# A four-layer graph kernel: attention prepared with Newton steps and early tiles, 64x64 maps in layer 2, biases moved to the head

## The chip, the cores and the metric

The kernel runs on one core of a Trainium2 chip. The metric is the device time of one execution in microseconds (us), taken as the median of three runs. Beside it stands one profiled execution, from which every duration of a single instruction comes.

## What is computed

Eight graphs (B) of 2048 nodes (N) with 64 features (F) pass through four residual layers that share one 0/1 adjacency matrix `adj` (2048 x 2048). Each layer first norms every node's features and clips them at zero. Cut to what matters here:

```
h = relu(layernorm(x))                      # before every layer
# layer 0: hyperedges and neighbours
industry = (adj / deg) @ (h @ W_ind)        # deg: row sums of adj
agg      = softmax over members (...) @ hW  # one vector per hyperedge
g        = weighted sum over a node's hyperedges of elu(mix of hW and agg)
x       += softmax-weighted mix of industry and g
# layer 1: graph attention
x       += elu(softmax(leaky(s_src + s_dst), masked by adj) @ hW)
# layer 2: three steps
v = relu(W1 [v, adj @ v] + b1);  v = W2 v + b2      # x 3, then x += v
# layer 3: Chebyshev terms and per-node weights
x += sum over k of T_k(adj) h @ w[node, k] + embedding @ bias
```

## The kernel before, in words

Two graphs are packed in one 128-partition tile (`half(0)` and `half(1)`), so there are four pairs `p`; nodes are cut in 16 tiles of 128 (`m`) or 4 chunks of 512 columns (`c`). TensorE (PE) does all contractions; a product with the adjacency is split in a rounded part and a rest (`hi`, `lo`), each one pass of 512 columns. Plain fp32 products appear as two instructions each.

The order of the work comes from three sources. Engines wrapped in `InOrder` (V, A, G, S for VectorE, ScalarE, GpSimd and SyncE) and all `kit.mm` while `kit.strict` is set keep the order of the program. Everything else is placed by the tile scheduler. In layers 2 and 3 a small planner (`Weave`) starts side chains when a planned time has passed.

The stages, with the lines of the profile:

- **Head of layer 0** (`layer0`, `step(j - lag)`): per node tile load `x`, norm on VectorE, GpSimd and ScalarE, transpose (L743), map with `W_ind` (L736 `py`), split, and `spread` the tile into four accumulators for chunk 0 of `industry`. Six 0.5 MB adjacency tiles `at` (L945, issued by GpSimd) are asked for before the loop.
- **Industry, chunks 1 to 3** (`industry`, `out_of`, `members`): 16 node tiles times 8 products `acc<-at,Y` (L1060). Between them, one per half tile, stand the `units`: the members of the hyperedges (`ph` L1115, copies `hi` L1119 and `lo` L1120, weights `es` L1123 to L1125, `hs` L1126, `pg` L1138), listings and, at the end, tables and the layer-3 biases (`pb` L1225, copy L1227). The row sums of the adjacency are added up on VectorE (`ds`, L1068), which the scheduler places; after the last product they are summed over partitions (`deg`, L1080), inverted with Ln and Exp (L1087, L1088) and multiplied into the copied accumulators (`ev`, L1075, L1091).
- **Pairs** (the loop `for j in range(last + 2 * NB)`): 54 steps over node and hyperedge pairs. VectorE does `mix`, `mix + pa` and `ex`, ScalarE an Exp, GpSimd the weighting (`weighed`), PE the products `pd`, `pa`, `pgs`. Before the loop stand the first tile's `ranks`, `edges`, `turn`, `shares` and the copies of the input into `x1_dram`.
- **Output of layer 0** (16 chunks; `first`, `second`, `third`, `differ`, `fourth`): two products with `fcW` (`pf`, 64-row tiles), Tanh to `th_s` (1024 columns), their difference, a product `pd` (64-column tiles), Tanh, and the mix `df`, which is added to `x1_dram` by an accumulating DMA for `p` over 0. `iv` (L1477) is loaded back from `ind_dram`; three 1 MB accumulating DMAs `xd<-hn` (L1536) add `gT`. Between these steps `first_neighbours` prepares pair 0 of layer 1: mean, variance (Square, PE, Ln, Exp), maps `ph`, scores, row factors `R`.
- **Attention, layer 1** (`attend`): per pair, half and node tile two VectorE passes `pt` (L1739, 128x1024), then 8 products `o` and 4 products `dn` on 32-column tiles. The next pair's preparation is woven in.
- **Layers 2 and 3** (`layers23`): per pair three steps of four chunks; each chunk is one map of `v` (`acc<-v,W1v` or `acc<-v,Wvc`, 128x128 stationary matrix with two equal 64x64 blocks on its diagonal), then 32 passes `acc<-aT,parts` (`spread`), a ReLU (L2089), and the map `py` for the next step (`carry`, `moved`). Then layer 3 with `u` (64-row tiles) and the reductions on VectorE.

Of the kernel before, what the change touches and what calls it, by code (L numbers as in the profile page):

```python
# [16 lines left out]
P = 128  # L17
# [602 lines left out]
LN_EXP = "natural_log_exp_and_others"  # L620

# [14 lines left out]
class Kit:  # L636


    def __init__(self, tc, t, pool):
# [11 lines left out]
        self.eps = pool.tile([P, 1], FP, name="eps_f")  # L651
        nc.vector.memset(self.eps, EPS)

        self.tiny = pool.tile([P, 1], FP, name="tiny_f")
        nc.vector.memset(self.tiny, 1e-30)
# [117 lines left out]
def layer0(kit, hn, x1_dram, open_early, late_tile, between):  # L773
# [31 lines left out]
    rden = lst.tile([P, LT, B], FP, name="rden")  # L805

# [28 lines left out]
    with ExitStack() as sA:  # L835
# [35 lines left out]
        def listing(ps):  # L871
# [4 lines left out]
            def slots():  # L876
                tmp = lst.tile([P, SLOTS], mybir.dt.int32, tag="hhi", name="iota_i", bufs=3)
                nc.gpsimd.iota(tmp, pattern=[[1, SLOTS]], base=0, channel_multiplier=0)
# [3 lines left out]
                nc.gpsimd.iota(ti, pattern=[[1, P]], base=0, channel_multiplier=-1)  # L882
# [51 lines left out]
        sp = sA.enter_context(tc.tile_pool(name="streamf", bufs=6, reuse_waits="tile"))  # L934
# [16 lines left out]
        with ExitStack() as s1:  # L951
            sb = s1.enter_context(tc.tile_pool(name="nf_sb", bufs=2, reuse_waits="tile"))
            ps = s1.enter_context(tc.tile_pool(name="nf_ps", bufs=2, space=PSUM, reuse_waits="tile"))
            acc = accs()
# [9 lines left out]
            def sums(i):  # L964
                st[i] = sb.tile([P, 2, B], FP, tag="st", name="st", bufs=4)
                V.tensor_reduce(st[i][:, 0], groups(xs[i]), AX.X, OP.add)
                V.tensor_scalar(st[i][:, 0], st[i][:, 0], -1.0 / F, None, op0=OP.mult)
# [47 lines left out]
            for i in range(4):  # L1015
                load(i)
            for g in range(6):
                at[g] = rows_of(0, g)
            kit.strict = True
            for j in range(NT + 5):  # L1020
                on = lambda k: 0 <= j - k < NT
                if 0 < j and j + 3 < NT:
                    load(j + 3)
                if j == 6:
                    first = loads()
                for lag, step in (
# [3 lines left out]
                    if on(lag):  # L1030
                        step(j - lag)
                m = j - 5
                if m > 0 and m % 2 and m // 2 + 6 < NT // 2:
                    at[m // 2 + 6] = rows_of(0, m // 2 + 6)
# [6 lines left out]
        with ExitStack() as s1:  # L1041
# [7 lines left out]
            def industry(c, own):  # L1049
# [3 lines left out]
                acc, ds = accs(), dsp.tile([P, 2, CW], FR, tag="ds", name="ds")  # L1053
                for g in range(NT // 2):
                    at = rows_of(c, g)
                    for k in range(2):
# [10 lines left out]
                    if g > 0:  # L1067
                        nc.vector.tensor_tensor(ds, (was if g == 1 else ds).bitcast(FP), at.bitcast(FP), op=OP.add)  # L1068
                    was = at
                return out_of(c, acc, ds)  # L1070

            def out_of(c, acc, ds):
                ev = [sb.tile([P, CW], FP, tag="ev", name="ev", bufs=4) for p in range(NP)]
                for p in range(NP):
                    (nc.scalar.copy if p % 2 else nc.vector.tensor_copy)(ev[p], acc[p])  # L1075
                deg = ds
                if c:
                    deg = ps.tile([P, CW], FP, tag="ph", name="deg", bufs=2)
                    for k in range(2):
                        mm(deg, ones_r, ds[:, k, :], start=k == 0, stop=k == 1)  # L1080
                rdeg = sb.tile([P, CW], FP, tag="rdeg", name="rdeg", bufs=1)
                nc.vector.tensor_scalar(rdeg, deg, 1.0, None, op0=OP.max)
                nc.vector.tensor_reduce(bad[:, 3 + c : 4 + c], deg, AX.X, OP.min)
                nc.vector.tensor_scalar(bad[:, 3 + c : 4 + c], bad[:, 3 + c : 4 + c], 0.5, None, op0=OP.is_lt)

                def inverse():
                    nc.scalar.activation(rdeg, rdeg, AF.Ln, scale=2.0)  # L1087
                    nc.scalar.activation(rdeg, rdeg, AF.Exp, scale=-1.0)  # L1088

                def shares(p):  # L1090
                    nc.vector.tensor_mul(ev[p], ev[p], rdeg)  # L1091
                    nc.sync.dma_start(out=ind_dram[p, :, cols(c)], in_=ev[p])

                return [inverse] + [lambda p=p: shares(p) for p in range(NP)]

            def members(i):
# [4 lines left out]
                def begin():  # L1101
                    hi = sb.tile([P, BF_ + 2 * B], FR, tag="hi", name="hi")
                    lo = sb.tile([P, BF_ + 2 * B], FR, tag="lo", name="lo")
# [108 lines left out]
            bw = sb.tile([16, P], FP, name="bw", bufs=1)  # L1212
            for h in range(2):
                nc.sync.dma_start(out=bw[:, half(h)], in_=t["L3_gnn_bias"])

            def rows(c):
                e = kept[f"e{c}"] = sb.tile([16, CW], FP, tag="ev", name="eT", bufs=4)
                nc.sync.dma_start(out=e, in_=t["embT"][:, cols(c)])

            def biases(c):  # L1220

                e = kept[f"e{c}"]
                pb = ps.tile([P, 4, P], FP, tag="ph", name="pb", bufs=2)
                for k in range(4):
                    mm(pb[:, k, :], e[:, k * P : (k + 1) * P], bw, start=True, stop=True)  # L1225
                bs = sb.tile([P, CW], FP, tag="ev", name="bs", bufs=4)
                nc.scalar.copy(bs, pb.rearrange("p k n -> p (k n)"))  # L1227
                nc.sync.dma_start(out=kit.bias_dram[:, cols(c)], in_=bs)

# [226 lines left out]
    with ExitStack() as s0:  # L1456
# [80 lines left out]
        for _ in steps:  # L1537
            pass
# [727 lines left out]
```

## Time and profile before

| | us |
|---|---|
| median of 3 runs (lowest, highest) | 1931.26 (1929.91, 1939.18) |
| the profiled execution, whole | 1937.11 |
| its span, first to last instruction | 1935.3 |
| PE / VectorE / ScalarE / GpSimd busy in the span | 1868.5 / 1176.9 / 460.1 / 310.9 |
| granted PE clock, mean | 0.988 |

The profile lists busy times per engine, the waits of each engine with what ended them, the groups of like instructions, and a chain followed back from the last instruction. A stage table gives the busy time of each engine in a stretch of the span. PE's busy time counts matmuls with modelled ends, so "busy" is not "at its peak"; the spacing of starts is what a matmul really takes.

### The profile page before, as it was taken

The page shows a single profiled execution, that of the slowest core. Times are in us where ns is not written, and L with a number is a line of the kernel's source. Part 1 is how long each engine was busy: PE and PEld are TensorE (multiplying, and loading weights), DVE is VectorE, ACT ScalarE, POOL GpSimd, SP SyncE. Part 2 cuts the span into 40 slices and gives each one's busy share as a digit, 9 for nine tenths or more (in the row PEclk, how much of TensorE's full clock was granted, in tenths as well). Part 3 has the DMA queues.
Part 4 walks back from the last instruction along what each step waited for, and adds up shares of the span by engine and source line. Part 5 has one row for each costly group of instructions (what it writes and reads, how often), then busy time and mean ns, then how long its engine had stood idle before and what let it go on. Part 6 is the DMA issues. An engine that isn't in the chain of part 4 may idle for free.

```text
span 1935.3 us, 25629 instructions
## 1 busy us (share of the span) xinstructions
PE 1868.5 (97%) x10084; PEld 1142.5 (59%) x10084; DVE 1176.9 (61%) x1862; ACT 460.1 (24%) x1043; POOL 310.9 (16%) x435
## 2 busy tenths in 40 slices
PE   7999999878999999999999999999999999999997
PEld 6877777423323332248775568765577855687653
DVE  8675399767898988973327552446623266523465
ACT  6322355565313131111220101301112201012100
POOL 4111078411000000000002110111200022101122
PEclk9999899989999999999999999999999999999998
DMA  7656376374122212214101112101122011121000
GB/s 215 173 161 190 119 231 170 89 190 108 39 61 50 61 45 56 66 25 115 60 23 25 30 44 71 49 14 26 25 73 60 22 25 30 44 71 50 5 19 12
DMA packets 86371, 142.57 MB, mean 74 GB/s; under 512 B 33800, under 2 KB 34056, under 8 KB 83568
## 3 DMA queue, kind: packets, MB, share of 16 engines
q1 hardware_dynamic: 65200, 83.86, 14.9%
q0 software_dynamic: 21040, 56.98, 12.0%
q8 instruction: 81, 1.33, 0.3%
q14 instruction: 50, 0.41, 0.1%
HBM read 106.85 MB, written 37.09 MB: 74 GB/s over the span
## 4 chain that ended last, share of the span: by engine, by line
PE 73%; issue 15%; DMA 4%; DVE 3%; POOL 2%; ACT 1%; SPq 0%; POOLq 0%; DVEq 0%; ACTq 0%
PE acc L736 33%; PE u L736 15%; PE o L736 5%; PE py L736 3%; PE dn L736 2%; PE pd L736 2%; PE pgs L736 2%; PE acc L1060 2%; DMA iv<-ind_dram 1%; PE mean L736 1%; PE var L736 1%; DMA at<-in_adjT 1%; DVE pt L1739 1%; PE pm L736 1%; DMA den<-d_dram 1%
## 5 line engine op out<-in xcount | busy, mean ns | idle before, releaser
L736 PE MATMUL acc<-aT,parts 128*128 128x512 f32 x1664 | 455.8, 418 | 0.0
L736 PEld LDWEIGHTS acc<-aT,parts 128*128 128x128 f32 x1664 | 306.4, 188 | 107.1 <-issue 51.4
L1739 DVE SCALAR_TENSOR_TENSOR pt<-R,wd,aT 128x1024 f32<-128x1024 f32 x192 | 236.0, 1280 | 14.8 <-DMA R<-r_dram 5.6
L736 PE MATMUL u<-W3f,y 64*128 64x512 f32 x1024 | 241.7, 589 | 0.0
L2141 DVE TENSOR_TENSOR pr<-u,embf 128x512 f32<-128x512 f32 x256 | 170.6, 687 | 109.7 <-PE u L736 102.7
L736 PE MATMUL o<-pt,hS 128*32 128x512 f32 x2048 | 234.7, 593 | 1.7 <-DVE pt L1739 1.6
L736 PEld LDWEIGHTS u<-W3f,y 64*128 64x128 f32 x1024 | 100.8, 187 | 119.1 <-issue 119.1
L736 PEld LDWEIGHTS o<-pt,hS 128*32 128x32 f32 x2048 | 64.7, 110 | 155.6 <-issue 144.7
L736 PE MATMUL u<-W3f,v 64*128 64x512 f32 x512 | 133.5, 596 | 0.0
L2153 POOL TENSOR_TENSOR fold<-fold 128x256 f32<-128x256 f32 x64 | 47.7, 745 | 495.8 <-DVE fold L2152 495.8
L736 PE MATMUL dn<-pt,vd 128*32 128x512 f32 x1024 | 122.4, 595 | 0.0
L1957 DVE TENSOR_TENSOR yb<-py,cb_f 128x512 f32<-128x512 f32 x32 | 22.1, 691 | 159.7 <-PE py L736 159.7
L1060 PE MATMUL acc<-at,Y 128*128 128x512 f32 x384 | 106.3, 419 | 0.0
L736 PE MATMUL acc<-aTl,parts 128*128 128x512 f32 x384 | 98.2, 394 | 0.0
L2145 DVE TENSOR_TENSOR pr<-pr 128x512 f32<-128x512 f32 x128 | 88.1, 688 | 2.2
L2047 POOL TENSOR_TENSOR bq<-bq,xp 128x512 f32<-128x512 f32 x16 | 20.8, 1300 | 425.2 <-ACT xp L2030 425.2
L736 PEld LDWEIGHTS u<-W3f,v 64*128 64x128 f32 x512 | 56.6, 186 | 49.8 <-issue 36.4
L1739 DVE SCALAR_TENSOR_TENSOR pt<-R,wd,aTl 128x1024 f32<-128x1024 f32 x64 | 79.7, 1282 | 10.4 <-PE dn L736 6.2
L736 PEld LDWEIGHTS acc<-aTl,parts 128*128 128x128 f32 x384 | 71.4, 188 | 15.5
L1060 PEld LDWEIGHTS acc<-at,Y 128*128 128x128 f32 x384 | 71.3, 195 | 15.0 <-issue 1.3
L736 PEld LDWEIGHTS dn<-pt,vd 128*32 128x32 f32 x1024 | 30.8, 109 | 73.0 <-issue 69.0
L1971 DVE TENSOR_TENSOR parts<-tp,parts 128x512 fp32r<-128x512 f32 x16 | 11.1, 692 | 84.9 <-ACT parts L1970 84.9
(354 smaller groups left out, 2698.4 us busy)
## 6 DMA issues: line engine op xcount, KB each, us to landing
at<-in_adjT POOLq DMA_DIRECT2D x32, 512.0 KB, 5.3
raw<-in_adjT SPq DMA_DIRECT2D x64, 256.0 KB, 3.4
aT<-in_adjT POOLq DMA_DIRECT2D x12, 1024.0 KB, 5.9
xp<-xd SPq DMA_DIRECT2D x45, 256.0 KB, 3.0
R<-r_dram SPq DMA_DIRECT2D x14, 512.0 KB, 3.8
hlo<-lo_dram POOLq DMA_DIRECT2D x18, 235.1 KB, 3.8
hhi<-hi_dram POOLq DMA_DIRECT2D x18, 235.1 KB, 3.6
hi_dram<-hi SPq DMA_DIRECT2D x16, 264.0 KB, 3.1
```

The costliest lines, as they stand in the source:

```text
L736: one = self.nc.tensor.matmul(*args, **kw)
L1060: mm(acc[p], Y[h][:, m, p, :], at[:, k, :], start=m + h == 0, stop=m == NT - 1 and h == 1)
L1739: nc.vector.scalar_tensor_tensor(pt, R[b2], wd[:, m, b2 : b2 + 1], aT[m][:, s].bitcast(FP), op0=OP.max, op1=OP.mult)
L1957: nc.vector.tensor_tensor(yb, py, bias[:, None, :].to_broadcast([P, 4, P]), op=OP.add)
L1971: nc.vector.tensor_tensor(lo, tp, hi.bitcast(FP), op=OP.subtract)
L2047: nc.gpsimd.tensor_add(bq, bq, xp)
L2141: nc.vector.tensor_tensor(a, u[h], emb[:, i, 8 * w : 8 * w + 8, None].to_broadcast([P, 8, F]), op=OP.mult)
L2145: nc.vector.tensor_add(pr[h], pr[h], a)
L2153: nc.gpsimd.tensor_add(fold[:, :, 0:2, :], fold[:, :, 0:2, :], fold[:, :, 2:4, :])
```

## The change

1. **Head.** The biases of layer 3 (4 chunks of 4 small products, a ScalarE copy each, and their loads and stores) move from the end of the industry stage into the first steps of the head. Only two `at` tiles are asked for before the loop, three more in steps 1 to 3; the ring of `at` has 5 buffers instead of 6.
2. **Industry.** The row sums `ds` are added in program order, ahead of the products of their tile, and `deg` and its inverse are made before the last tile's products. So two of the four accumulators are scaled as they are copied, the other two after (for the last chunk on GpSimd). The tiles `hi` and `lo` of the members get three buffers.
3. **Start and end of the pairs.** `ident_r` is made early; node tile 1 is prepared and the Tanh table loaded before the first tile's steps; the copies into `x1_dram` go one by one into the loop at tiles 4, 8 and 12. The last two weightings are done by VectorE.
4. **Output of layer 0.** `iv` is fetched six to seven chunks ahead in 8 fixed buffers; the accumulating DMAs and the late adjacency tiles are issued in program order, the 1 MB ones at steps 3, 7 and 11. `th_s` uses the buffers of `pt`. Pair 0 of layer 1 follows a written plan: the variance is taken with two columns of the averaging matrix in the same tile as `ph`, and the inverse root comes from a bit guess and three Newton steps on VectorE (128x32), so Ln and Exp of the variance are gone. The `pt` of the first two node tiles are made here.
5. **Layer 2.** In steps 1 and 2 the maps of two chunks are made together as four products of 64x64 blocks on the four quarters of the array, after the first 8 node tiles of the even chunk. The odd chunk's halves are swapped on the way: its ReLU is two ScalarE instructions in steps 0 and 1, and its `carry` uses a swapped matrix `Wxc` and starts 0.5 later in the planner's time.

The core of the diff:

```diff
-        sp = ...tile_pool(name="streamf", bufs=6, ...)
+        sp = ...tile_pool(name="streamf", bufs=5, ...)
...
+            def biases(c):
+                for k in range(4):
+                    kit.mm(pbs[c][:, k * P : (k + 1) * P], eT[c][:, k * P : (k + 1) * P], bw, start=True, stop=True)
...
-            for g in range(6):
+            for g in range(2):
                 at[g] = rows_of(0, g)
...
+                for c in {1: (0, 1), 3: (2,), 4: (3,)}.get(j, ()):
+                    biases(c)
+                if 9 <= j < 9 + NCW:
+                    S.dma_start(out=kit.bias_dram[:, cols(j - 9)], in_=bs[j - 9])
+                if 1 <= j < 4:
+                    at[j + 1] = rows_of(0, j + 1)
...
+                    if g > 0:
+                        V.tensor_tensor(ds, (was if g == 1 else ds).bitcast(FP), at.bitcast(FP), op=OP.add)
+                    if g == NT // 2 - 1:
+                        rdeg = degrees(c, ds)
...
-                    if g > 0:
-                        nc.vector.tensor_tensor(ds, (was if g == 1 else ds).bitcast(FP), at.bitcast(FP), op=OP.add)
...
+                        nc.vector.tensor_mul(ev[p], acc[p], rdeg)
+                        store(p)
...
-                    hi = sb.tile([P, BF_ + 2 * B], FR, tag="hi", name="hi")
+                    hi = sb.tile([P, BF_ + 2 * B], FR, tag="hi", name="hi", bufs=3)
...
+            weigh = V if j > last - 3 else G
...
+        next_nodes(1)
+        tc.keep_in_program_order(nc.scalar.preload_act_table_set(TANH_EXP))
...
+                if i in (4, 8, 12):
+                    S.dma_start(out=x1_dram[i // 4], in_=t["xT"][i // 4])
...
+        def fetch(i):
+            p, c = chunks[i]
+            ivs[i] = io.tile([P, CW], FP, tag=f"iv{i % 8}", name="iv")
+            S.dma_start(out=ivs[i], in_=ind_dram[p, :, cols(c)])
...
+            if 0 < i and i + 6 < len(chunks):
+                fetch(i + 6)
-            if i in (1, 4, 8):
+            if i in (3, 7, 11):
                 p = 1 + i // 4
-                nc.gpsimd.dma_start(out=x1_dram[p], in_=gT[p], accum_op=OP.add)
+                G.dma_start(out=x1_dram[p], in_=gT[p], accum_op=OP.add)
...
+        def newton():
+            V.tensor_tensor(nw, rstd, rstd, op=OP.mult)
+            V.scalar_tensor_tensor(nw, nw, -0.5, var, op0=OP.mult, op1=OP.mult)
+            V.scalar_tensor_tensor(rstd, nw, 1.5, rstd, op0=OP.add, op1=OP.mult)
...
+            ("DVE", 16, lambda: self.edge(0, 0, V)), ("V2", 16, lambda: self.edge(0, 1, V)),
+            ("DVE", 17, lambda: self.edge(1, 0, V)), ("DVE", 17, lambda: self.edge(1, 1, V)),
...
+    def quarters(accs, W, c):
+        for d in range(2):
+            for h in range(2):
+                mm(accs[d][half(h ^ d)], W[half(h), half(h)], v[half(h), cols(c + d)], start=d == 1, stop=False)
+        weave.passed(0.6)
...
-        yield 1.4
-        yn[c] = moved(v, c, Wec, cb, None if step else LENT[c])
+        yield 1.9 if c % 2 else 1.4
+        yn[c] = moved(v, c, Wxc if c % 2 else Wec, cb, None if step else LENT[c])
...
-                mm(acc, Wvc if step else W1v, v[:, cols(c)], start=True, stop=False)
-                weave.passed(0.93)
-                spread(acc, y, c, False, every)
+                elif c % 2 == 0:
+                    spread(acc, y, c, True, range(0, 8))
+                    quarters(accs, Wvc, c)
+                    spread(acc, y, c, False, range(8, NT))
+                else:
+                    spread(acc, y, c, False, every)
...
+                if step < 2 and c % 2:
+                    for h in range(2):
+                        nc.scalar.activation(v[half(1 - h), cols(c)], acc[half(h)], AF.Relu, bias=b[half(h)])
```

## The prediction

> **What bounds the kernel now.** I read the page first, then the stage table (us of stretch, then busy time of PE, PE's weight loads, VectorE (DVE), ScalarE (ACT), GpSimd (POOL), granted clock, DMA share, GB/s), then the waits, then single rows.
>
> ```profile
> 0.00:20.00 20.00, 8.21 (x43) 7.09 (x44) 13.99 (x42) 9.17 (x28) 10.94 (x19) 1.00 0.90 277
> 20.00:70.00 50.00, 50.00 (x298) 43.95 (x297) 35.91 (x65) 30.09 (x103) 16.67 (x19) 1.00 0.59 146
> 70.00:118.00 48.00, 45.77 (x235) 35.95 (x234) 38.43 (x119) 11.92 (x45) 5.58 (x8) 1.00 0.64 192
> 118.00:166.00 48.00, 43.31 (x218) 33.68 (x218) 28.00 (x106) 11.06 (x40) 8.46 (x12) 0.96 0.59 174
> 166.00:230.00 64.00, 60.81 (x310) 48.41 (x310) 28.18 (x76) 15.68 (x38) 3.37 (x5) 0.95 0.35 109
> 230.00:237.00 7.00, 3.58 (x20) 2.71 (x19) 5.73 (x11) 4.67 (x10) 1.23 (x1) 0.87 0.87 301
> 237.00:366.00 129.00, 129.00 (x593) 92.80 (x591) 119.49 (x188) 68.68 (x175) 95.72 (x109) 0.95 0.61 176
> 366.00:375.20 9.20, 5.68 (x22) 2.37 (x20) 5.89 (x9) 4.07 (x14) 4.85 (x4) 1.00 0.02 8
> 375.20:466.30 91.10, 69.74 (x274) 26.40 (x273) 54.31 (x81) 58.94 (x83) 15.32 (x19) 0.93 0.74 178
> 466.30:852.00 385.70, 383.30 (x3200) 116.20 (x3203) 348.43 (x306) 82.64 (x227) 19.35 (x28) 1.00 0.21 52
> 852.00:1935.30 1083.30, 1069.13 (x4890) 732.98 (x4882) 498.55 (x865) 163.15 (x283) 129.44 (x212) 1.00 0.15 41
> ```
>
> PE bounds head, attention (466 on) and layers 2 and 3 (852 on): there only fewer PE passes help. The pairs (237 to 366) are VectorE's, 93% busy. Idle PE sits in the first 12 us, in the industry stage (70 to 230: 10.1 us), at 230 to 237, in the pairs' tail, and above all in layer 0's output (91.1 us, 21.4 of them idle). The waits name the causes (total, times, longest):
>
> ```profile
> PE ph L1115 <- DVE hs L1126: 8.9, 5, 3.5
> PE pf L736 <- DMA iv<-ind_dram: 8.6, 4, 2.6
> PE pf L736 <- ACT th_s L631: 4.2, 1, 4.2
> DVE ds L1068 <- DMA at<-in_adjT: 12.6, 6, 3.8
> ```
>
> In the industry stage VectorE, in order, sits in `ds` for a tile that has only been asked for, and PE's `ph` waits for the `hs` queued behind. In the output, `iv` is late behind the three 1 MB accumulating DMAs.
>
> Rows for layer 2 and two moved pieces (groups, then PE's timeline):
>
> ```profile
> L1225 PE MATMUL pb<-bw,eT 16*128 16x128 f32 x32 | 4.6, 283 | 0.0
> L631 ACT ACT_TABLE_LOAD x4 | 5.1, 1283 | 0.1
> ```
>
> ```profile
> 905.40 1.02 PE L736 MATMUL acc<-v,Wvc_f 128*128 128x512 f32 x2
> 905.85 1.02 PE L736 MATMUL acc<-aT,parts 128*128 128x512 f32 x2
> 906.71 1.05 PE L736 MATMUL py<-Wec_f,v 128*128 128x128 f32 x8
> ...
> 1031.04 1.89 PE L736 MATMUL u<-W3f,y 64*128 64x512 f32 x8
> 1032.86 0.74 PE L736 MATMUL acc<-aT,parts 128*128 128x512 f32 x2
> ```
>
> From 905.40 to 906.71 stand one map and two passes of 0.229: a map costs 1.31 - 0.46 = 0.85. `u` shows two 64-row tiles side by side: 8 instructions of 0.427 each take four slots, 1.72, so they end at 1032.76, and the next full-array product starts 0.10 later. Attention's `o` packs four column tiles (32 instructions in 3.43).
>
> [...] 0.10 leaving `u`, 0.19 entering it at 1043.04. [...] here the granted clock is 0.50 to 0.62 from 235 to 250, after the idle at 230.
>
> **The change, part by part** (against the profiled execution, 1937.1, 1.8 of it outside the span; the median is 5.8 lower, and I subtract from it).
>
> *Head: -1.* GpSimd issues two `at` instead of six (0.7 each) before `xc(0)`, so that step starts about 1 earlier, and fewer bytes compete with `x`. Added before PE's first transpose (idle until 10.0): two bias chunks of 8 instructions[...], two more of about 1.1 in steps 3 and 4, where PE still waits for the norm; four ScalarE copies of 0.6 beside 46% busy. Six loads join SP's and ACT's queues ahead of `x(1)`, four stores join SP's later. If `eT` comes late, PE's in-order transpose waits: +3 to -3. With five `at` buffers a tile has four tile times of over 6 us to land, median 5.3: nothing.
>
> *Industry: -12.* (a) The 4 bias chunks leave a stretch where PE is full: 4 x 1.08 = 4.3. (b) `ds` stands ahead of the products of its own tile, so VectorE no longer waits for tiles that PE doesn't need yet; with three `hi`/`lo` buffers the wait for their stores (3.1 in all) goes too. Of PE's 8.9 I take 7 away; the additions of 1.22 stay, under PE. (c) The clock dips after those waits, and `deg` moves under the products: 1. Bounds -5 and -15. VectorE is 38.4 of 48 busy in chunk 1, so a rest of the wait may stay.
>
> *Start of the pairs: -3.5.* `mix(0)` started at 235.0, 5.5 after the last product. Off that path go `rdeg` by Ln and Exp, the four multiplies (2.5), `ident_r`, the table load of 1.28 (now behind the copies but ahead of `be`) and the wait for `sT(1)` (2.0). Left: two scaled copies 1.4, `oT` 0.55, `pm`, `be`: about 3.4, so 2 gained[...]. GpSimd's two multiplies (about 1.3 each) have slack; the three `x1_dram` copies leave the crowded stretch (DMA 0.87) for one of 0.61, where the features have a tile time (7.3) against 3.6 to land. Bounds -1 and -5.
>
> *End of the pairs: -1.6.* GpSimd's last three weightings run 368.8 to 372.6, 1.27 each; VectorE does two at 0.69 right behind `ex`.
>
> *Output of layer 0: -18.* PE's work is 16 x 2.93 (steps at 405.4, 408.4) = 47, means 4, `ph` 4.6 plus 32 tiny products (in place of `var`, 4) that I put at 0.11, the spacing of the small `pm` at 232, rows 3.9: 63. ScalarE loses four table loads (5.1) and Ln, Exp (4.8) and gains eight `hS` copies of about 0.37: 52 left. VectorE: 54.3 less 5.9 (`xc`, `hS`) plus clip and copies 3, Newton and scores 14 x 0.18 = 2.5 (the small `es` and `sc` rows take 0.15 to 0.16), `hS` 0.7, four `pt` of 1.28 = 5.1: 60. So PE and VectorE are close; chunks 0 to 3 cost VectorE 4.0 a step (+4), Newton is one dependent stretch (+2), the last `pt` another 2 to 3, the prologue 2. I take 73 instead of 91. Perfect overlap is 67 (-24). Against it: the DMA work (0.74 of 91 = 67 us of the full share) hardly shrinks and must hide in 73; if the share shows work and not queueing, little is won: -8. GpSimd's queue is now in order: a `df` addition waits for the 1 MB one of its pair, and `fetch(i+6)` in SP's queue waits for chunk i-2's `df` to land, SP's later stores behind it.
>
> *Attention's start: -2.* Four `pt` are ready, so PE's two waits (1.6) and thin packing to 470 go. `scaled`, 3 x 0.69, is added under a VectorE with 10% slack; bounds 0 and -3.
>
> *Layer 2: -8.* Sixteen times two maps (1.71) become four quarters. All four together: 0.85 plus two drains (0.29) plus the first weight load, about 1.2: 16 x 0.5 = 8. Bounds: no drain, -13.7; quarters only two at a time (2.0), +4.8. The extra ReLU (0.6) and the 0.5 later `carry` are covered: before, the last chunk's `lo` ends at 900.8 and PE needs it at 903.6; 2.8 less 0.6 leaves 2.2.
>
> Sum: 1 + 12 + 3.5 + 1.6 + 18 + 2 + 8 = 46; 1931.3 - 46 = 1885.
>
> **Rivals.** *Quarters in turns*[...]: the new part does nothing; +4.8 for -8 gives 1898. [...] *Output bound by transfers*: -8 for -18, with waits for `iv` left: 1895. For: the share of 0.74; against: from 405 to 410 PE was full with a share of 0.36. *Slower: late fetches.* Place: steps 7 to 15, where a fetch waits for a `df` addition that sits behind a 1 MB one. A fetch has five steps of 3.9 = 19.5. The 1 MB additions landed in 17.4, and the longest `iv` piece of the chain was 21.6, together 39: three fetches, 19.5 late each, +58: 1943. It decides once landing and fetch exceed 35 (three times 15.5 eats the 46). Against: 17.4 was three at once; now they are spaced, four steps apart.
>
> **Numbers.** Forecast 0.63, quarters 0.14, transfers 0.15, slower 0.04, the rest (all bounds poor, near 1924) 0.04. Measurement tells 0.5% (9.7 us) from no change. Forecast's own range 1871 to 1897; to hold 8 in 10 with the next two cases: 1870 to 1905. Faster 0.93, same 0.03, slower 0.04.
>
> **What would show it.** Right: no PE wait of `ph` on `hs` over 2; the first `o` near 430 instead of 466.3 (1 + 12 + 3.5 + 1.6 + 18 earlier); the output 70 to 76 long; the eight `Wvc` instructions within 1.2; the later stage 8 shorter. Wrong: PE waits on `iv` or `th_s` over 5, an output over 80, quarters spaced over 1.7, PE waits on `parts` at step ends.

## The result and the profile after

The changed kernel takes 1916.31 us (median of 4 runs, 1914.77 to 1916.65) against 1933.15 of the kernel before on the same chip (4 runs, 1929.91 to 1939.18). The ratio is 0.9908, with a 95% interval of 0.9887 to 0.9930: a gain of 0.9%, about 17 us, where 46 were forecast. The profiled execution took 1914.77, its span is 1913.0; the span of before was 1935.3, so the two traces differ by 22.3 (the profiled run of before lay near the top of its range).

The stage table after, with the columns of the one before (busy PE, weight loads, VectorE, ScalarE, GpSimd, clock, DMA share, GB/s):

```profile
0.00:24.00 24.00, 14.40 (x73) 12.60 (x74) 12.85 (x41) 10.64 (x32) 9.54 (x16) 1.00 0.74 215
...
170.00:225.60 55.60, 53.51 (x251) 42.84 (x250) 30.89 (x71) 13.47 (x32) 3.62 (x6) 0.88 0.29 93
...
237.00:246.00 9.00, 0.78 (x4) 0.78 (x4) 4.33 (x6) 0.72 (x1) 5.64 (x8) 0.76 1.11 331
...
374.80:440.60 65.80, 62.60 (x299) 26.73 (x300) 52.39 (x87) 49.27 (x69) 13.20 (x16) 1.00 0.80 179
```

The hole of before at 230 is gone, and the output's row shows PE busy for 62.6 of 65.8. A new hole has opened at 237: nine microseconds in which PE works for 0.78 and the DMA share is over 1. PE's waits name it and the others (total, times, longest):

```profile
PE pm L737 <- DMA hlo<-lo_dram: 8.2, 1, 8.2
PE o L737 <- DVE pt L1793: 5.2, 1, 5.2
...
PE acc L737 <- DMA eT<-in_embT: 3.6, 1, 3.6
...
PE deg L1119 <- DVE ds L632: 2.4, 2, 2.1
...
PE py L737 <- ACT v L2203: 1.7, 1, 1.7
```

A wait for `bw` (4.1) and a second one of `py` (1.0) belong to the same causes as their neighbours. The waits that the prediction wanted gone are gone (`ph` on `hs`, `pf` on `iv` and on `th_s`), down to 0.4 or less each. In the kernel before, PE had none of the five waits shown at more than 1.0; in its head it waited 10.0 for the first `xc` instead. By stage, from one PE event to the next in both traces:

| stage | before | after | difference | forecast |
|---|---|---|---|---|
| head, to the first `acc<-at,Y` | 19.4 | 23.9 | +4.5 | -1 |
| industry, to the end of its last product | 210.3 | 201.7 | -8.6 | -12 |
| pairs, to the first `pf` | 145.5 | 149.2 | +3.7 | -5.1 |
| output, to the first `o` | 91.1 | 65.8 | -25.4 | -18 |
| attention, to the end of the last `o` | 391.9 | 398.5 | +6.6 | -2 |
| layers 2 and 3, from the first `acc<-aT` | 1074.0 | 1070.9 | -3.1 | -8 |
| sum | | | -22.3 | -46 |

Three stages moved against the forecast. Each new wait is followed to its source below.

### The profile page after: what moved, and what is told of

Its sections match the earlier page's. It is cut to its first block, busy times and chain, and to the rows that moved or that the text cites. A ratio compares the mean times of both kernels' runs of the same rounds, so it can differ in the third digit from the quotient of the medians.

```text
span 1913.0 us, 25771 instructions
## 1 busy us (share of the span) xinstructions
PE 1860.1 (97%) x10172; PEld 1135.7 (59%) x10172; DVE 1176.0 (61%) x1869; ACT 464.2 (24%) x1048; POOL 314.9 (16%) x435
## 4 chain that ended last, share of the span: by engine, by line
PE 72%; issue 15%; DVE 5%; DMA 5%; POOL 2%; ACT 1%; SPq 0%; POOLq 0%; DVEq 0%; ACTq 0%
PE acc L737 32%; PE u L737 14%; PE o L737 5%; PE acc L1098 3%; PE py L737 3%; PE dn L737 3%; PE pgs L737 2%; PE pd L737 2%; DVE pt L1793 1%; PE var L737 1%; PE mean L737 1%; PE pv L737 1%; PE pm L737 1%; DMA hlo<-lo_dram 1%; DMA den<-d_dram 1%
## 5 line engine op out<-in xcount | busy, mean ns | idle before, releaser
L737 PE MATMUL acc<-aT,parts 128*128 128x512 f32 x1664 | 441.4, 409 | 0.0
L1793 DVE SCALAR_TENSOR_TENSOR pt<-R,wd,aT 128x1024 f32<-128x1024 f32 x188 | 230.7, 1279 | 21.0 <-DMA R<-r_dram 13.9
```

The source lines that it names most:

```text
L737: one = self.nc.tensor.matmul(*args, **kw)
L1793: V.scalar_tensor_tensor(pt, R, w, a.bitcast(FP), op0=OP.max, op1=OP.mult)
```

## The experiments

All are compared with the kernel before, run on the same chip. They ran on several chips, so two of them are compared with each other by their ratios to it. Effects of 2 to 7 us are too small for the total alone, so the stage is read from the profile too. Over the six profiles whose head and industry stage are those of the changed kernel, the first adjacency product came at 23.2 to 26.4 and the last one ended at 221.7 to 226.3; over those with the stage unchanged, the pairs took 148.2 to 150.1, the output 65.4 to 66.7, attention 397.8 to 399.5, layers 2 and 3 1069.0 to 1070.9. A difference inside such a spread is not read. Each stage of a run is read from one trace.

### Attention: a row factor that lies on live memory (e1_rfactor)

VectorE, SyncE (SPq) and PE in the trace of the changed kernel, at the last half of pair 2 and the first of pair 3 (start, length, in brackets the idle time ahead and what ended it):

```profile
714.93 22.41 SPq L1782 DMA_DIRECT2D R<-r_dram  x2
...
741.57 8.53 DVE L1793 SCALAR_TENSOR_TENSOR pt<-R,wd,aT 128x1024 f32<-128x1024 f32 x7 [8.45 <-DMA R<-r_dram]
742.91 2.77 PE L737 MATMUL o<-pt,hS 128*32 128x512 f32 x10 [5.17 <-DVE pt L1793]
```

The two loads of R are neighbours in the queue, and their issue takes 22.4 together: the second goes at 737. SyncE's own waits say for what it stood, first in the changed kernel, then in the one before:

```profile
SPq L1782 <- PE o L737: 21.7, 1, 21.7
```

```profile
SPq L1868 <- PE o L736: 21.2, 1, 21.2
```

In the kernel before, the same wait for PE's last `o` belonged to a later load (`xp`, L1868), for which nobody waited. The change moves the `pt` pool to the other side of memory and adds tiles to the pool next to it. The profile shows no addresses. But `o` does not read R, so I take the wait to mean that the second late R buffer now lies on a tile that pair 2's last `o` still reads. The experiment gives that load other memory:

```diff
-        r = (self.sb2 if self.turn % 3 == 0 else self.R).tile(..., bufs=2 - (self.turn % 3 == 0))
+        lone = self.turn in (3, 6, 9, 14)
+        r = (self.sb2 if lone else self.R).tile(..., bufs=2 - lone)
```

> The changed kernel with the row factors R of the last pair placed otherwise: the second R of the first half takes the single buffer of the attention pool, the first R of the second half takes the late buffer in its place. Theory (the late buffer lies on memory that the last products o of pair 2 still read, so its load is issued only after them): SyncE issues both R loads within 2 us of each other, VectorE's wait for R of 8.5 us and PE's wait for pt of 5.2 us there vanish, the step from the seventh to the previous Ln of dn (55.7) returns to about 50, and the kernel is about 6 us faster than the changed one, near 1910. Rival (the load is late because it stands behind other transfers, or one profile caught an accident): the wait stays near 5, the time within 2 us of the changed kernel.

Measured: 1906.64 (ratio 0.9857, 0.9824 to 0.9890); attention 391.7. SyncE in that trace:

```profile
715.19 0.80 SPq L1783 DMA_DIRECT2D R<-r_dram  x2
```

Both loads go at once, VectorE and PE have no such wait left, and attention is 6.8 shorter. The theory holds. The 6.8 are more than PE's wait of 5.2: in the changed kernel the granted clock was 0.50 from 740.0, inside that wait, to 746.8, and PE was busy for 3.89 of it; half of that, 1.9, is my estimate of what it cost. In e1 and in the kernel before the clock is 1.00 there.

### Pairs: copies that nobody holds back (e2_copies)

SyncE, GpSimd and PE of the changed kernel after the last industry product:

```profile
228.26 1.81 SPq L632 DMA_DIRECT2D xd<-in_xT  x3
...
231.62 0.56 POOL L820 DMA_DIRECT2D hlo<-lo_dram  x1
...
245.22 0.38 PE L737 MATMUL pm<-hlo,sT 114*128 114x16 f32 x1 [8.24 <-DMA hlo<-lo_dram]
```

The copies into `x1_dram` stand in the source at node tiles 4, 8 and 12, but SyncE has nothing to wait for between them: all three, 1 MB read and 1 MB written each, are issued within 1.8 us of 228.26. `hlo`, asked for at 231.62, lands 13.6 later (the median of all its loads in this trace is 3.7).

```diff
                 if i in (4, 8, 12):
-                    S.dma_start(out=x1_dram[i // 4], in_=t["xT"][i // 4])
+                    A.dma_start(out=x1_dram[i // 4], in_=t["xT"][i // 4])
```

> The changed kernel with the three 1 MB copies of the input into x1_dram issued from ScalarE's queue at the same places of the program (node tiles 4, 8, 12) instead of SyncE's. Theory (SyncE has nothing to wait for between them, so it issued all three at 228 us and they slow the load of hlo): the copies start some 29 us apart, the wait of pm for hlo (8.2 us at 237) falls under 2, and the stretch from the last industry product to the first pf falls from 149 to about 141; the kernel gains 6 to 8, near 1909. Rival (hlo is late because GpSimd's two multiplies and the 1 MB adjacency tile stand ahead of it in its queue): the wait stays at 5 to 8 and the stretch at 146 to 149.

Measured: 1904.39 (ratio 0.9847, 0.9818 to 0.9876); pairs 142.9. ScalarE's queue has work between them, and there they are spread:

```profile
258.65 0.59 ACTq L632 DMA_DIRECT2D xd<-in_xT  x1
...
317.23 0.50 ACTq L632 DMA_DIRECT2D xd<-in_xT  x1
```

The wait for `hlo` is 0.2; the load asked for at 229.4 lands 5.5 later. GpSimd's two multiplies and the adjacency tile still stand ahead of it in the queue, so the rival is out.

### Layer 2: a matrix on memory that a DMA still reads (e3_wxc, e5_quarters)

VectorE, ScalarE and PE of the changed kernel where layer 2 begins:

```profile
857.68 0.17 DVE L2160 MEMSET Wxc<- 128x128 f32 x1 [8.51 <-DMA xd<-e]
...
859.53 0.69 DVE L2046 TENSOR_TENSOR yb<-py,cb_f 128x512 f32<-128x512 f32 x1
860.25 0.62 ACT L2048 CAST parts<-yb 128x512 fp32r<-128x512 f32 x1 [9.51 <-DVE yb L2046]
...
862.34 1.16 PE L737 MATMUL py<-Wxc,v 128*128 128x128 f32 x8 [0.98 <-ACT v L2201]
```

Read upward: `py` waits for the ReLU (860.90), the ReLU stands behind a cast on ScalarE, the cast waits for `yb`, `yb` stands on VectorE behind the clearing of `Wxc`, and that waits for the last accumulation of attention (`xd<-e`). No value of `e` goes into `Wxc`, so I take it that `Wxc` was put where `e` lay.

```diff
-    nc.vector.memset(Wxc, 0.0)
+    nc.gpsimd.memset(Wxc, 0.0)
     for h in range(2):
-        nc.vector.tensor_copy(Wxc[half(h), half(1 - h)], Wec[half(h), half(h)])
+        nc.gpsimd.tensor_copy(Wxc[half(h), half(1 - h)], Wec[half(h), half(h)])
```

> The changed kernel with the swapped matrix Wxc cleared and filled by GpSimd instead of VectorE. Theory (Wxc takes memory under the last accumulation of attention, so its clearing holds VectorE until 857.7, and yb, the cast of parts and the ReLU of v behind it are late): VectorE's 8.5 us before Wxc vanish, PE's waits of py for v (1.0 and 1.7) fall to under 0.5 in all, the stretch from the first product with aT to the end shortens by 2.5 (1071 to 1068.4). Rival (the two ReLU instructions of the odd chunk and the later carry make py late): the waits stay at 2 to 2.7.

Measured: 1911.49 (0.9877, 0.9848 to 0.9906); layers 2 and 3 1068.5. PE at the same place:

```profile
859.68 1.05 PE L737 MATMUL py<-Wxc,v 128*128 128x128 f32 x8
```

`yb` runs at 850.7 instead of 859.5, and the waits of `py` fall from 2.7 to 0.3. The total alone would not show it (the interval overlaps that of the changed kernel); the chain does. Then the layer-2 part alone, in the kernel before, with `Wxc` filled in this way:

> The kernel before with the layer-2 part of the change alone (maps of two chunks as four 64x64 products, swapped ReLU and carry; Wxc is filled by GpSimd). Theory (a group of quarters costs 1.2 against 1.71 for two maps, but each group loses another 0.07 to 0.1, so 16 groups save 6.9, and only pair 0 gives some back): the stretch from the first product with aT to the end falls by 6 to 7 from 1074.0, the time by 0.3% to about 1927 where before is near 1934. Rival (the layer-2 part is worth about 3, as the changed kernel's 1070.9 reads): the stretch falls by 2 to 4.

Measured: 1928.18 (0.9952, 0.9927 to 0.9978); layers 2 and 3 1067.6 instead of 1074.0, 6.4 less. The quarters in the trace of the changed kernel:

```profile
883.56 1.62 PE L737 MATMUL acc<-aT,parts 128*128 128x512 f32 x6
885.11 1.09 PE L737 MATMUL acc<-v,Wvc_f 64*64 64x512 f32 x8
886.13 0.50 PE L737 MATMUL acc<-aT,hi 128*128 128x512 f32 x1
```

Six passes of 0.229 would end at 884.93; the next full-array product starts at 886.13. So four products on the quarters cost 1.20, as forecast. (The "drains" in the forecast are two gaps in the trace of before, 0.10 ahead of 1032.86 and 0.19 ahead of 1043.04; what PE does in them is not shown.) But from one such group to the next in step 1 it is 17.79, where two chunks of before took twice 9.08: a gain of 0.37, not 0.5. Where the other 0.14 went was not traced.

### Head: loads that displace `x`, and slow products (e4_xfirst, e9_later, e12_back)

PE and VectorE in the first microseconds of the changed kernel:

```profile
4.07 2.04 PE L737 MATMUL acc<-bw,eT 16*128 16x128 f32 x8 [4.07 <-DMA bw<-in_L_gnn_bias]
9.73 2.07 PE L737 MATMUL acc<-bw,eT 16*128 16x128 f32 x8 [3.62 <-DMA eT<-in_embT]
...
10.29 0.69 DVE L632 TENSOR_REDUCE st<-x 128x8 f32<-128x512 f32 x1 [5.87 <-DMA x<-in_xN]
```

Two candidates: x(1), issued at 3.6 behind `eT` and weights, came 5.9 late for VectorE; and PE's bias products wait for their loads (`bw` 4.1, then `eT`) ahead of the first transpose, which starts at 13.34 instead of 10.04. First the order of the loads:

```diff
-            load(0)
+            for i in range(2):
+                load(i)
...
-                (A if c > 1 else S).dma_start(out=eT[c], in_=t["embT"][:, cols(c)])
+                A.dma_start(out=eT[c], in_=t["embT"][:, cols(c)])
```

> The changed kernel with the second x tile asked for right behind the first, and all four eT loads on ScalarE's queue behind bw. Theory (x(1) was issued at 3.6 behind two eT loads and two weight loads and landed at 10.2, and the sums of x(1) stand ahead of the second sums of x(0) on VectorE): sums of x(1) near 4.5 instead of 10.3, first acc product of the adjacency near 20.5 instead of 23.9, kernel 3 to 3.5 faster. Rival (PE's bias products, which wait for bw and eT ahead of the first transpose, set the time): x(1) early but first acc product still at 23 or later, gain under 1.

Measured: 1912.08 (0.9879, 0.9850 to 0.9909). The sums of x(1) start at 4.3 and the first transpose at 12.2, but `eT` is waited for 8.2 in all, and the first adjacency product comes at 22.9, only 0.3 ahead of the spread: the rival is nearer, and x(1) alone is worth 1 at most. Then the products behind the transpose as well (the copies on ScalarE move with them):

```diff
-                for c in {1: (0, 1), 3: (2,), 4: (3,)}.get(j, ()):
+                for c in {3: (0, 1), 4: (2, 3)}.get(j, ()):
```

> The changed kernel with x(1) asked for right behind x(0), all eT loads on ScalarE's queue, and the bias products moved behind the first transpose: two chunks ahead of the first map, two ahead of the second. Theory (what PE's in-order queue waits for ahead of its first transpose, the loads of bw and eT, set the head once x(1) is early): first tpx near 10 as in the kernel before, first acc product of the adjacency near 22 (19.4 plus some of the 5.6 that the products take), kernel 2 to 4 faster than the changed one. Rival (the products cost their own 5.6 wherever they stand ahead of the first spread): first acc product at 23 to 25, no gain over the run with x(1) early alone.

Measured: 1911.40 (0.9876, 0.9849 to 0.9903), and what the rival forecast came:

```profile
9.43 3.78 PE L737 MATMUL acc<-bw,eT 16*128 16x128 f32 x16
...
24.34 1.86 PE L737 MATMUL acc<-at,Y 128*128 128x512 f32 x7
```

The transpose starts at 8.38, 1.7 earlier than in the kernel before, the products then take 3.78 twice, and the adjacency comes at 24.3. Everything on PE is slow here: in the changed kernel the eight instructions of `py` take 2.08 at 16.39 and 1.06 at 26.02. (The column of the granted clock reads 1.00 for the head because that trace's clock record begins at 19.75.) Last, the biases back at the end of the industry stage:

> The changed kernel with the biases made at the end of the industry stage again, as before (products, copies, loads and stores). Theory ([...] their loads hold back x(1)): the first adjacency product comes near 19.5 to 20.5 instead of 23.3 to 26.4, the stretch up to the last industry product grows by 4 to 5 from about 200 to 204.5, and the whole is within 2 us of the changed kernel. Rival (the forecast: the head hides the biases, its delay comes from elsewhere, such as the at tiles asked for one by one): first product at 23 or later and the kernel 4 slower.

Measured: 1915.57 (0.9891, 0.9875 to 0.9908), level with the changed kernel. The first adjacency product comes at 19.9, so the 4 to 5 of the head are the biases. The industry stage is 201.3, inside the 197.8 to 201.7 of the six profiles without them, and its last product ends at 221.2; the next part says why this does not make the biases free there.

### Industry: what ended the waits for `hs` (e10_sched, e11_twobufs, e14_both, e16_front)

The first edit (e10) lets the scheduler place the additions; the second (e11) takes the third buffer of `hi`, and likewise of `lo`; e14 does both.

```diff
-                        V.tensor_tensor(ds, ...)
+                        nc.vector.tensor_tensor(ds, ...)
...
-                    hi = sb.tile([P, BF_ + 2 * B], FR, tag="hi", name="hi", bufs=3)
+                    hi = sb.tile([P, BF_ + 2 * B], FR, tag="hi", name="hi")
```

> The changed kernel with the additions of row sums ds placed on VectorE by the scheduler again instead of in program order (their source text stays ahead of the products). Theory (the order of ds is what removed PE's 8.9 of waits for hs): waits of ph for hs of 4 to 9 come back, the industry stage grows by 4 to 8 from about 151. Rival (the third buffer of hi and lo and the biases' leaving did it): waits for hs under 2, stage within 2 us, and PE's waits of deg for ds (1.4 to 2.4) stay or grow.

Measured: 1913.36 (0.9893, 0.9865 to 0.9920); stage 196.9. VectorE waits 10.4 for `at` in `ds` again, and PE's `ph` does not wait for `hs` at all. My theory missed.

> The changed kernel with two buffers of the members' tiles hi and lo again instead of three. New theory (the third buffer is what ended PE's waits for hs, since they stayed away with ds placed by the scheduler): waits of ph for hs or of PE for member work of 4 or more come back and the stretch from the first adjacency product to the last industry product grows from about 200 to 204 or more. Rival (the five at buffers, asked for one by one, or the biases' leaving ended them): waits under 2, stretch within 2 of 200.

Measured: 1912.29 (0.9882, 0.9861 to 0.9904); stage 199.1, no wait for `hs`. The new theory missed too.

> The changed kernel with ds placed by the scheduler and two buffers of hi and lo (both parts undone). If the two parts cover for each other: PE's waits for hs or other member work come back with 5 or more, the stretch from the first adjacency product to the last industry product grows from about 200 to 204 or more. If what ended them is something else (the five at tiles asked for one by one, two multiplies less on VectorE at the head of a chunk): waits under 2, stretch 197 to 200.

Measured: 1917.45 (0.9927, 0.9910 to 0.9943); stage 202.5, waits for member work 1.6 at most. Neither part, nor both, bring the 8.9 back. What these three left in place, among other things, is that the text of the additions stands ahead of the products of their tile. So the additions in program order at that place, nothing else, in the kernel before:

```diff
                     at = rows_of(c, g)
+                    if g > 0:
+                        V.tensor_tensor(ds, ...)
+                    was = at
                     for k in range(2):
...
-                    if g > 0:
-                        nc.vector.tensor_tensor(ds, ...)
-                    was = at
```

> The kernel before with the row sums ds in program order ahead of their tile's products, nothing else changed. Theory (order alone is enough): waits of ph for hs fall from 8.9 to under 3, the industry stretch (first adjacency product to last, 210.3) shortens by 5 or more, time near 1929. Rival (order alone isn't enough, the member tiles' buffers hold VectorE): waits stay over 5.

Measured: 1926.80 (20 runs; 0.9969, 0.9956 to 0.9982); stage 200.6 instead of 210.3 (207.2 in e5, whose stage is that of before too). PE's largest waits between 68 and 228 are now these, and the longest for `hs` is 0.6:

```profile
PE px L736 <- POOL sT L826: 2.0, 1, 2.0
...
PE ph L1115 <- DVE rank L915: 1.3, 1, 1.3
```

So the additions in program order at that place are enough; buffers and biases are not needed for it.

The length of the stage has three parts that the traces keep apart: PE's idle time, what half clock costs, and the rest, PE's work at full clock. In the clock records of these traces the granted clock is 1.00 or 0.50. In the changed kernel a pass `acc<-at,Y` takes 0.47 at 0.50 (four from 176.11 to 177.98) and 0.24 at 1.00 (eight from 23.87 to 25.79), so half of the time at 0.50 is put down as its cost. The whole stage before, after, with the biases back (e12), and with these and other edits (e15, below):

```profile
19.36:229.71 210.35, 200.24 (x1058) 162.33 (x1057) 130.89 (x365) 68.86 (x227) 34.08 (x43) 0.98 0.53 151
23.87:225.58 201.71, 197.50 (x1028) 160.64 (x1027) 132.95 (x364) 67.90 (x226) 35.88 (x47) 0.97 0.55 160
19.94:221.23 201.29, 197.81 (x1060) 160.58 (x1059) 132.90 (x362) 69.96 (x229) 35.83 (x47) 0.99 0.56 160
19.68:226.17 206.49, 203.78 (x1060) 166.10 (x1059) 132.39 (x364) 70.26 (x229) 35.69 (x47) 0.96 0.55 156
```

| us | stage | idle | half clock | rest |
|---|---|---|---|---|
| before | 210.3 | 10.1 | 5.1 | 195.1 |
| e16, place of `ds` alone | 200.6 | 2.7 | 3.4 | 194.4 |
| changed kernel | 201.7 | 4.2 | 6.8 | 190.7 |
| e10 | 196.9 | 2.9 | 3.4 | 190.6 |
| e12, biases back | 201.3 | 3.5 | 1.7 | 196.1 |
| e15 | 206.5 | 2.7 | 8.5 | 195.2 |

The rest is 190.5 to 191.2 in all twelve traces without the biases and 194.4 to 196.1 in all five with them. So the biases cost this stage about 4 us, and e12's length hides that, because its half clock is the least of all seventeen. In the traces of before and of the changed kernel the stretches at 0.50 last 3.41, 6.83, 10.24 or 13.65 us, but for the last one of each, in which the span ends; so half clock is counted in steps of 3.41 here, and the stage has from one (e12) to five (e15). In every trace a stretch of one to three steps begins 0.5 to 4.3 us after the first of 36 small products `pn` (8 columns each), and no wait of PE over 0.3 stands in the 5 us before it; in the changed kernel:

```profile
207.70 4.16 PE L1256 MATMUL pn<-ea,MT 64*114 64x8 f32 x36
...
210.90:217.70 6.80, 6.80 (x20) 5.52 (x20) 4.89 (x5) 0.00 (x0) 0.00 (x0) 0.50 0.00 0
```

That these products bring it about was not tried.

### Output: spacing and Newton (e7_accum, e13_lnexp)

The 1 MB accumulations at steps 1, 4 and 8 again:

> The changed kernel with the three 1 MB accumulating DMAs of layer 0's output issued at steps 1, 4 and 8, as in the kernel before, instead of 3, 7 and 11. Theory (the waits for iv went because fetches and accumulations were spread out): PE's waits for iv come back with 5 or more, the output stretch (first pf to first o) grows from 65.8 to 72 or more. Rival (the output is shorter because the fixed buffers let SyncE fetch eight chunks ahead, and because Ln, Exp and their table loads left ScalarE): iv waits stay under 2 and the stretch within 2 us of 65.8.

Measured: 1912.21 (0.9880, 0.9856 to 0.9903); output 65.4, no wait for `iv`. Spacing them is worth nothing here; what the rival names in its place was not tried by this run. Then Ln and Exp of the small tile in place of guess and Newton steps:

> The changed kernel with the inverse root of pair 0 by Ln and Exp of ScalarE on the same 128x32 tile, instead of the bit guess and three Newton steps on VectorE. Theory (Newton's steps matter for the table loads that they save, two of 1.28 here, on a path with little slack): two more table loads, output stretch 2 to 4 longer than 65.6. Rival (the gain of the output lies in the small tile and in the plan, the chain of Newton's steps being as long as Ln, Exp and the loads): within 1.5 of 65.6.

Measured: 1914.01 (0.9890, 0.9861 to 0.9919); output 68.3. ScalarE pays for two table loads (424.35 and 425.98), and PE waits 2.1 for the `th_s` behind them:

```profile
424.35 1.28 ACT L632 ACT_TABLE_LOAD   x1
...
428.56 2.08 PE L737 MATMUL pf<-iv,fcWf 64*128 64x512 f32 x4 [2.09 <-ACT th_s L632]
```

Newton's steps are thus worth 2.5 to 2.9 of the 25.4 (1.6 against the longest output of the others, 66.7). The other 22 were not taken apart by a run. The two traces say only of what they consist: PE's idle time fell from 21.4 to 3.2, and the half clock of before (13.7 us of it, which cost 6.8) is gone; PE's work at full clock is 62.9 before and 62.6 after.

### The repairs together (e8_best, e15_best)

> The changed kernel with five repairs together: R of the last pair in another buffer (6.8 in its run), x1_dram copies on ScalarE's queue (6.4), Wxc by GpSimd (2), ds placed by the scheduler (3), x(1) asked for first (1.5). If they add, it is 19 to 20 faster than the changed kernel, near 1896 to 1898. If one repair uncovers the next wait, less: 1901 to 1905.

Measured: **1894.34** (0.9783, 0.9764 to 0.9802), 22 less than the changed kernel (24 by the ratios): head 24.6, industry 199.1, pairs 140.7, output 65.4, attention 391.9, layers 2 and 3 1067.8. The three repairs of waits (R, copies, `Wxc`) show in their stages; the two in head and industry do not.

> The changed kernel with R of the last pair in another buffer, x1_dram copies on ScalarE's queue, Wxc by GpSimd, ds placed by the scheduler, and the biases back in the industry stage. Theory[...]: last industry product near 219 instead of 223.7, time near 1890. Rival (both places cost the same, about 4.5): last industry product at 223 to 225, time 1894 to 1896.

Measured: 1898.62 (0.9824, 0.9807 to 0.9842). The head is back at 19.7, but the industry stage takes 206.5, and its last product ends at 226.2. The theory missed, and the time is over the rival's too. By the table above the stage holds the biases again (195.2) and five steps of half clock, the most of any trace. By the ratios this kernel is 0.4% slower than e8, so in this company the biases do better in the head.

## Why the prediction was wrong

The direction was right and the size was not: 17 instead of 46. The traces fall 23.8 short of the sum of the steps. The largest parts are attention (8.6), the pairs (8.8) and the head (5.5); the output gave 7.4 more than forecast, which hides as much of the rest. The steps that failed are the head's, the copies' in the pairs and the clock's in the industry stage; for the R load and for `Wxc` the sum had no term. By the prediction's own steps:

**Head, -1: wrong, +4.5.** The step "two more of about 1.1 in steps 3 and 4, where PE still waits for the norm" failed, and so did the place given to the two ahead of the first transpose. The chunks took 2.0, 2.1, 2.1 and 1.4 (1.08 from one start to the next at 216.29 in the kernel before), the first two came only when `bw` and `eT` had landed, and PE did not wait for the norm in steps 3 and 4. Its bound of +3 was for a late `eT` alone; e9 shows that with no wait for `eT` the head is as long (24.3), by the products alone. With the biases out of the head the first adjacency product is back at 19.7 to 19.9.

**Industry, -12: -8.6 in the trace.** Term (a), the biases' 4.3, is right: PE's work at full clock fell by 4.4. But the head took as much, 4.5, so in the changed kernel the move gained nothing (e12). Term (b), the place of `ds`, is confirmed by itself: e16 gains 6.6 to 9.8 in the stage with it alone; in the changed kernel PE's idle time fell by 5.9, of 7 forecast. Its reason is only half right: in e10 VectorE waits for `at` again and PE doesn't suffer. That what counts is where the additions stand among the members' work is a guess that fits all four runs. Term (c) failed: instead of gaining 1, the clock cost 1.7 more. The two dips of before behind waits for `hs` (0.50 for 3.4 each from 136.0 and from 183.8, the waits 3.5 and 2.0) are gone, but one came anew and one grew. `deg` in PE's queue waited 2.1 for the last addition, the clock was 0.50 from 173.3 to 180.2, and the half clock at `pn` lasted two steps instead of one. With 4.4, 5.9 and -1.7 the 8.6 are complete. The runs without the biases take 196.9 to 202.5, and the table's idle time (2.4 to 5.1) and half clock (3.4 to 6.8) make up the difference; what decides how many steps a run gets is open.

**Start of the pairs, -3.5, and their end, -1.6: wrong by one step.** "The three `x1_dram` copies leave the crowded stretch" is what failed: they were issued at 228.26. With the copies really spread, the pairs take 142.9, 140.7 and 142.1 (e2, e8, e15), against 145.5 - 5.1 = 140.4 forecast. The rest of the two steps may stand, but no run took it apart; of the start's 3.5, all beyond the 2 that the shorter path gives was an estimate of mine.

**Output, -18: right in kind, too small; -25.4.** PE's work was put at 63 and PE is busy for 62.6; VectorE's 60 became 52.4. The surcharges for imperfect overlap (4 + 2 + 2 to 3 + 2) were nearly all unnecessary: the stage runs within 3.2 of PE's busy time. Some of it was pushed over the line, though: from the first `o` to the first `ds<-dn` it is 53.6 instead of 51.8. The part of the earlier fetches was not tried by itself; e7 shows only that their spacing from the accumulations does not matter.

**Attention's start, -2: wrong, +1.8,** since of "four `pt` are ready" one was, at the first `o` (VectorE made the others from 441.4 to 445.1, between mixes of the output). And the prediction had no step at all, so nothing, for what cost 5.9 later, the R load on memory in use (6.8 by e1): the diff said only that a pool changes sides.

**Layer 2, -8: mechanism right, -3.1.** Quarters cost 1.20 as forecast; in full they gave 6.4 (e5), not 8, because a pair of chunks gained 0.37 to 0.4. The "covered" ReLU and carry were covered; what was not was the new tile `Wxc`, whose clearing the prediction did not price. It took back 0.5 to 2.3: e3's 1068.5 stands against 1069.0 to 1070.9 in all runs with VectorE's `Wxc`.

Rivals: quarters in turns did not occur (1.20 a group, where two at a time were put at 2.0). Waits for `iv` neither stayed nor returned with the old spacing, so neither the transfer bound nor the late fetches did. The R load, the copies and `Wxc`, which no rival named, cost 6.8, 6.4 and 0.5 to 2.3 in their stages, and the head 5.5 against its step. The first three have one form: an instruction was judged by its length and its place in the source, and not by what its queue or its memory makes it wait for.

## What to carry to other kernels

Three DMAs at node tiles 4, 8 and 12 were issued within 1.8 us from SyncE's queue, which had nothing to wait for between them, and at 258.65 to 317.23 from ScalarE's, which had work there. So their place in the program did not spread them; the queue's work did. When a change moves a pool or adds a tile, ask for every first write into it which earlier reader, DMAs included, still holds that memory, and what is queued behind the writer: a load that was harmless at the end of such a wait can become the one that everybody needs (SyncE waited 21.2 before and 21.7 after; PE behind it not at all and 5.2). Work moved into an idle stretch is free only if its inputs are there before the stretch ends and the engine runs at its full pace there; a chunk's eight instructions took up to 2.1 in the head and 1.1 where they came from. And before a stage's length in one trace is put down to an edit, its half clock is taken out: that alone moved the industry stage by up to 6.8 between these runs.

## What the runs showed of the hardware

Three waits of PE in the changed kernel went with a lower granted clock: for `hlo` (8.2), R (5.2) and `ds` (2.1). The clock was 0.50 for 10.2 us from 241.6 and for 6.8 from 740.0, both inside the wait, and for 6.8 from 173.3, 0.5 after it. Behind the last, a pass took 0.47, about twice the 0.24 of the eight at 23.87:

```profile
172.88 0.80 PE L1119 MATMUL deg<-ds,ones_r 128*128 128x512 f32 x2 [2.09 <-DVE ds L632]
...
176.11 2.07 PE L1098 MATMUL acc<-at,Y 128*128 128x512 f32 x4
```

The length of the wait alone does not tell: in the kernel before, one of 3.2, longer than that for `ds`, was followed by no such stretch (the clock is 1.00 from 426.1 to 1924.6), and at `pn` one comes with no wait over 0.3 in the 5 us ahead. What sets it off is not shown.

```profile
451.85 1.17 PE L736 MATMUL ph<-W1x,xc 128*128 128x132 f32 x8 [3.16 <-DVE xc L631]
```

Four 64x64 products with two instructions each take 1.20 from the end of the pass ahead to the start of the pass behind (884.93 to 886.13), where a single 128x128 map takes 0.85 (905.40 to 906.71 in the kernel before, less two passes) and two at a time would take 2.0 (the prediction's estimate: four slots of 0.427 and the two gaps, 0.29). So the two that write different halves of one accumulator ran side by side here. Three 1 MB copies issued within 1.8 us, beside a 1 MB load, went with a landing time of 13.6 us for a 235 KB load; with the copies elsewhere the same load took 5.5.
